# Two-layer graph attention on one core: the first weights' logit columns made by TensorE, the overflow flag computed between the last products, the last graph stored in pieces

## The chip, the cores and the metric

The kernel runs on one core of a Trainium2 chip. The metric is the device time of one launch in microseconds (us); lower is better. It is given as the median of several runs. Beside it stands one profiled execution, whose trace is what this document reads.

## The reference

There are 64 graphs of 256 nodes with 512 features each, an adjacency matrix of zeros and ones for each graph, and two residual layers. Everything is float32. Cut to what matters:

```python
# layer 0: two GAT layers inside (4 heads of 256, then 1 head of 512)
h  = relu(layernorm(x))
xl = (h @ W1).reshape(B, N, 4, 256)
a  = einsum(xl, att_src1); b = einsum(xl, att_dst1)      # one logit per node and head
e  = leaky_relu(a[source] + b[destination]); e = where(adj > 0 or diagonal, e, -1e9)
h  = elu(softmax(e, over sources) applied to xl + b1)    # 256 x 1024
...  the same with W2 (1024 x 512), one head, + b2
x  = x + h
# layer 1: one GAT layer with 8 heads of 64, softmax over neighbours, relu
h  = relu(layernorm(x));  xp = h @ W_proj
x  = x + relu(softmax(leaky_relu(a_src + a_dst + b_att), masked) @ xp)
```

A logit `einsum(xl, att)` of a head is linear in `h`, so it equals `h @ (W1_head @ att_head)`. The kernel computes the small vectors `W1_head @ att_head` once and puts them beside the weights as extra columns, the logit columns, so that a product gives the logits together with the features. For the first weights there are 4 source and 4 destination columns of 512 values.

## The kernel before

**Stages of a graph.** Each graph passes through products with W1 (`m1a` for heads 0 and 1, `m1b` for heads 2 and 3), attention (`gat1`), ELU, the product with W2 (`m2`), attention (`gat2`), a second normalization, the product with W_proj (`m3`) and attention (`gat3`). All of it is written as short named steps, and three strings `head`, `order` and `tail` list them in an order written out by hand: an entry such as `-1 m1a p6` is step `p6` of product `m1a` of graph r-1, and `w dots2 5` is a step on the weights. `head` runs once, `order` runs for r = 2 to 62, `tail` runs once with r = 64. Every engine gets its instructions in exactly this order and executes them in order; waits come only from data and from buffers.

**Products.** A product is done in seven smaller products of quarter matrices (`p1` to `p7`, class `Product`), which need sums and differences of the blocks of both sides. The sums on the side of the nodes are made by `left` on GpSimd (POOL), those of the weights by `right` on VectorE (DVE), once in the head (`sums1`, `sums2`, `sums3`). The steps `q1`, `q6`, `q7` copy a PSUM sum away on ScalarE (ACT), and `q2`, `c22`, `q3` add on VectorE and `q4` copies on ScalarE into `xl1`, `xl2` or `xl3`. A 128 x 512 PSUM tile for results comes from the pool `ps_mm` (name `pm`, four buffers); running sums come from `ps_sum` (two buffers).

**Logit columns of the first weights.** `dots1 0` to `dots1 7` on VectorE make 32 dot products of a weight block of 256 columns with an attention vector that was read from HBM into all 128 partitions. Each writes one column of `w1a_sb`. These columns ride only in `m1a`; `m1b` has none. `sums1 0` needs them; `sums1 1` does not. `dots2` and `dots3` make the columns of the other two weights.

**Attention.** `exp1` makes exponentials of the logits, `ship1` transposes them and sends them to HBM, `rows1` reads them back into all partitions (tile `bc`), `edges1` builds the attention matrix of a head with two ScalarE scalings into `wys` and two VectorE operations into `e`, `gat1` multiplies it with the features, and `out1` divides by the sum. Layers 2 and 3 have the same steps. The last graph does not go through HBM: `spread_at_once` makes the rows on TensorE.

**Turning.** TensorE needs the node features with the feature index on the partitions. Graph 0 is turned by TensorE (`turn0`), later ones through HBM (`away`, `home`) and VectorE (`back`); the last graph is turned by TensorE again in layer 3 (`back3` calls `turn`).

**Queues.** SyncE (SP) issues nearly all DMAs in order. ScalarE issues six of them at the start, and its two for the last two quarters of `w1a_sb` stand behind the normalization (`norm1`) in its queue. Every DMA signals on one of eight semaphores in turn, and a later DMA on the same semaphore is not issued until the earlier one has landed.

**The end.** `out3` divides on VectorE and adds into `x2` on GpSimd; `store` writes 512 KB for a graph. `range` keeps the largest and smallest exponential of a graph in `ends`. After the last step VectorE reduces `ends`, two tiny TensorE products sum over the partitions, and `flags` is written. All engines then read `flags` and branch around a slower general path, which is not taken with these inputs. The lines of the flag:

```python
    nc.vector.tensor_scalar(top[:, 3:4], top[:, 1:2], 1.0 / FAR, None, ALU.is_lt)
    pf = ps_mm.tile([P, 512], F32, name="pm")
    nc.tensor.matmul(pf[:2, 0:1], top[:, 2:4], ones, start=True, stop=True)
```

Of the kernel before, what the change touches and what calls it, by code (L numbers as in the profile page):

```python
# [110 lines left out]
def short_path(ctx, tc, flags, x, adj, w1, att_src1, att_dst1, b1, w2, att_src2, att_dst2, b2, w_proj, w_att,  # L111
# [51 lines left out]
    wp_sb = const.tile([P, 7, DC // 2, L3 + Q], F32, name="wp_sb")  # L163
    b1_sb = const.tile([P, HF], F32, name="b1_sb")
# [129 lines left out]
    class Graph:  # L294
# [264 lines left out]
        def out3(self, a, t):  # L559
            pv = self.pms.pop((3, a, t))[:, :G * (K3 + 1)].rearrange("p (h k) -> p h k", h=G)  # L560
            r = small.tile([P, G, 1], F32, name="r3")
            nc.vector.reciprocal(r, pv[:, :, K3:])
            o = work.tile([P, G, K3], F32, name="o", bufs=4)
            nc.vector.scalar_tensor_tensor(o, pv[:, :, :K3], 0.0, r.to_broadcast([P, G, K3]), ALU.max, ALU.mult)  # L564
            to = self.x2[:, t, a * Q:(a + 1) * Q]
            nc.gpsimd.tensor_tensor(to, to, o.rearrange("p h k -> p (h k)"), ALU.add)  # L566
# [5 lines left out]
        def store(self):  # L572
            nc.sync.dma_start(out[self.b].rearrange("(t p) d -> p t d", p=P), self.x2)
# [21 lines left out]
    def dot(dst, u, v):  # L595
        prod = work.tile([P, Q], F32, name="prod", bufs=2)
        nc.vector.tensor_tensor_reduce(prod, u, v, 1.0, 0.0, ALU.mult, ALU.add, dst)  # L597

    att1 = [work.tile([P, H1, F1], F32, name="x2", bufs=3) for i in range(2)]
# [4 lines left out]
    nc.scalar.dma_start(att1[0].rearrange("p h f -> p (h f)"), rows_of(att_src1, HF))  # L604
    for r in range(2):
        bring(w1_sb[1], w1, 2 * Q, r, (nc.sync, nc.scalar))
    nc.scalar.dma_start(att1[1].rearrange("p h f -> p (h f)"), rows_of(att_dst1, HF))
# [19 lines left out]
    class Weights:  # L627


        def __init__(self):  # L630

            self.dots = sorted(((r, s, h, c) for s in range(2) for r in range(2) for h in range(H1) for c in range(2)),
                               key=lambda d: (d[2] < 2, d[0] > 0 or d[2] % 2 == 0, d[1]))
            self.sums = {}

        def dots1(self, i):
            for r, s, h, c in self.dots[4 * i:4 * i + 4]:
                dot(blocks(w1_sb[0])[r][s][:, c, h:h + 1], blocks(w1_sb[h // 2])[r][h % 2][:, c, -Q:], att1[s][:, h, :])
# [5 lines left out]
        def dots2(self, i):  # L644
            r, c = i // 4, i % 4
            for s in range(2):
                for half in range(2):
                    dot(va2[:, i, s, half:half + 1], blocks(w2_sb)[r][half][:, c, -Q:],
                        att2[s][:, half * Q:(half + 1) * Q])
# [27 lines left out]


    head = """
        0 turn0, w dots1 0, w dots1 1, 0 m1b p2, w dots1 3, 0 m1b p1, w sums1 1, w dots1 4, w dots1 5, w dots1 6,  # L680
        0 m1a p1, w dots1 2, w dots1 7, 0 m1a p2, w dots2 1, 1 load, w dots2 3, w sums1 0, 0 m1a q1, 0 m1b q1,
        w dots2 0, 0 m1b p6, 0 m1a p5, 0 m1a q2, 0 m1b p5, w dots2 7, w load3, 0 edge01, 0 masks, 0 m1a p6,
        1 stats1 0, 0 m1b q6, 0 m1a q6, 0 m1a p7, 0 m1a q7, 0 m1a c22, w dots2 2, 0 m1a p3, 0 m1a q3, 0 m1a p4,
        0 m1b p7, 0 caps, w dots2 6, 0 m1a q4, 0 exp1, 0 ship1, w dots2 4, 1 stats1 1, w dots2 5, 0 m1b q7,
        0 rows1, w columns2, 0 m1b c22, 1 norm1 0, 1 norm1 1, 1 away1, w sums2 0, 0 m1b q2, 0 open, w sums2 1,
        0 edges1 1, w sums2 2, 0 m1b p3, 0 m1b p4, 0 cap3, 0 edges1 0, 0 gat1 1 1, 0 gat1 1 0, 0 out1 1 0,
        0 gat1 0 0, 1 home1, 0 gat1 0 1, 0 edges1 2, 0 out1 1 1, 1 edge01, 0 m1b q3, 1 masks, 0 out1 0 0,
        1 back1 0, 0 ez1 0 0, 1 m1b p1, 0 out1 0 1, w sums2 3, w dots3 1, 0 elu1 0 0, 1 caps, 0 m1b q4, 1 m1a p1,
        1 back1 1, 0 gat1 2 1, 0 gat1 2 0, w dots3 0, 2 load, 0 edges1 3, 0 ez1 0 1, 0 elu1 0 1, 0 gat1 3 1,
        0 out1 2 1, 0 out1 3 1, w dots3 2, 0 send2 0 0, 0 out1 2 0, 0 gat1 3 0, 0 out1 3 0, 1 m1a q1, 1 left1,  # L690
        1 m1a p6, 0 send2 0 1, 1 m1a p5, 1 open, 0 take2 0 1, 1 m1b q1, 0 ez1 1 1, 1 m1a p2, 1 m1a q6, 0 elu1 1 1,
        1 m1a q2, w dots3 5, 1 m1b p6, 1 m1a p7, 0 ez1 1 0, 0 send2 1 1, w dots3 7, 0 elu1 1 0, 1 m1b q6, 1 m1a q7,
        0 take2 0 0, 1 m1b p2, 1 m1b p7, 1 m1a c22, 1 m1a p3, 1 m1a p4, w dots3 4, 0 back2 0 1, 0 take2 1 1,
        0 send2 1 0, 1 m1a q4, 1 m1b p5, 0 back2 0 0, 1 m1b q7, 0 back2 1 1, 1 cap3, w dots3 3, 1 m1a q3,
        0 take2 1 0, 1 exp1, 1 ship1, 1 m1b p4, 0 m2 p1, 0 m2 q1, w dots3 6, w sums3 0, 0 back2 1 0, 1 m1b q4,
        0 left2, 0 m2 p5, 2 stats1 0, 1 m1b q2, 0 m2 p6, 2 edge01, 0 again, 1 m1b c22, 0 m2 p2, 1 rows1,
        2 stats1 1, 2 masks, 0 m2 q6, w sums3 1, 1 edges1 1, 0 m2 p7, 0 m2 q2, 1 edges1 0, 1 gat1 1 0, 1 gat1 1 1,
        0 m2 q7, 1 out1 1 1, 0 m2 p4, 0 m2 c22, 2 norm1 0, 0 m2 p3, 2 norm1 1, 1 m1b p3, w sums3 2, 1 out1 1 0,
        1 edges1 2, 1 gat1 0 1, w sums3 3, 0 m2 q4, 0 m2 q3, 2 caps, 1 edges1 3, 2 away1, 1 gat1 0 0, 0 exp2,
# [355 lines left out]
```

## Time and profile before

| what | value |
|---|---|
| median of 3 runs | 2969.14 us (2966.99 to 2972.52) |
| the profiled execution, its own time | 2968.22 us |
| its span in the profile | 2966.4 us |
| mean granted TensorE clock | 0.996 |
| TensorE (PE) busy | 2917.8 us, 98% of the span |
| VectorE (DVE) busy | 2531.3 us, 85% |
| ScalarE (ACT) busy | 1711.3 us, 58% |
| GpSimd (POOL) busy | 1287.4 us, 43% |

Times in the profile count from the start of the span. "Busy" is the time in which an engine executed something; an engine that is not busy is waiting or has nothing to do. A matrix product of float32 appears as two records for each instruction of the program. The columns of the views are named where they are shown.

### The profile page before, as it was taken

Reading aid. Unit: us, or ns where it says so; the run is one execution under the profiler, and the core shown is the slowest. Engines: PE = TensorE matmul, PEld = TensorE weight load, DVE = VectorE, ACT = ScalarE, POOL = GpSimd, SP = SyncE. Lnnn points to the kernel's source line nnn. Section 1 sums busy time; section 2 is a strip of 40 time slices with the busy share of each in tenths; the row PEclk is TensorE's granted clock in tenths of the full one; section 3 lists DMA queues with packets and bytes.
Section 4 is the critical chain, followed back from the end, with each engine's and each line's share of the span. In section 5 each row is a group of like instructions: output and inputs, shape, how many; then the busy total and the mean of one; then the engine's idle time right before and its main releaser. Section 6 shows DMA issues by size and latency. Waiting matters only on the chain.

```text
span 2966.4 us, 59522 instructions
## 1 busy us (share of the span) xinstructions
PE 2917.8 (98%) x20296; PEld 2531.6 (85%) x20296; DVE 2531.3 (85%) x6370; ACT 1711.3 (58%) x4489; POOL 1287.4 (43%) x1882
## 2 busy tenths in 40 slices
PE   6999999999999999999999999999999999999997
PEld 4888888888888888888888888888888888888886
DVE  8788888888888888888888888888888888888886
ACT  3466565655655655655656556556556556555554
POOL 3443443444444444434444444444444344344433
PEclk9999999999999999999999999999999999999998
DMA  6556555656565665555556565565555556566542
GB/s 193 155 173 180 175 180 171 180 178 179 170 182 176 175 180 174 172 180 177 179 171 185 173 179 173 178 184 167 175 177 174 178 178 179 172 182 176 179 136 73
DMA packets 536859, 513.17 MB, mean 173 GB/s; under 512 B 85736, under 2 KB 373352, under 8 KB 536552
## 3 DMA queue, kind: packets, MB, share of 16 engines
q1 hardware_dynamic: 535176, 507.20, 57.5%
q8 instruction: 165, 2.70, 0.4%
q10 hardware_dynamic: 1376, 2.10, 0.2%
q14 instruction: 142, 1.16, 0.1%
HBM read 332.01 MB, written 168.79 MB: 169 GB/s over the span
## 4 chain that ended last, share of the span: by engine, by line
PE 97%; DVE 1%; DMA 1%; issue 0%; ACT 0%; POOL 0%; SPq 0%; ACTq 0%; DVEq 0%
PE sum L55 38%; PE pm L55 29%; PE pm L411 15%; PE pm L556 8%; PE pm L481 7%; DVE prod L597 0%; DMA w1a_sb<-in_L_gnn_W_dram 0%; DMA xs<-in_x_dram 0%; DMA h<-kept_h 0%; DMA z<-kept_z 0%; DVE e L292 0%; DVE hs L213 0%; ACT h L199 0%; DVE z L419 0%; DMA bc<-kept 0%
## 5 line engine op out<-in xcount | busy, mean ns | idle before, releaser
L291 ACT ACTIVATE wys<-bc,exs_sb 128x256 f32<-128x256 f32 x1646 | 715.4, 468 | 297.4 <-DMA bc<-kept 145.4
L61 ACT ACTIVATE kept<-sum 128x260 f32<-128x260 f32 (+3 forms) x768 | 296.0, 386 | 714.0 <-PE sum L55 713.3
L292 DVE SCALAR_TENSOR_TENSOR e<-wys,exs_sb,cap 128x256 f32<-128x256 f32 x1024 | 444.9, 476 | 62.2 <-ACT wys L291 52.6
L55 PE MATMUL sum<-w_sb,h1s 128*128 128x257 f32 x2048 | 488.1, 380 | 0.6
L411 PE MATMUL pm<-xl,e 128*128 128x257 f32 x2048 | 476.4, 380 | 0.9 <-DVE e L292 0.8
L411 PEld LDWEIGHTS pm<-xl,e 128*128 128x128 f32 x2048 | 387.9, 190 | 60.1 <-DVE e L292 1.7
L55 PEld LDWEIGHTS sum<-w_sb,h1s 128*128 128x128 f32 x2048 | 383.3, 190 | 64.3 <-issue 3.8
L566 POOL TENSOR_TENSOR x<-x,o 128x256 f32<-128x256 f32 x256 | 182.0, 731 | 486.5 <-DVE o L564 484.6
L261 DVE TENSOR_TENSOR xl<-pm,kept 128x256 f32<-128x256 f32 (+2 forms) x768 | 318.1, 415 | 79.1 <-ACT kept L61 40.4
L219 POOL TENSOR_TENSOR hs<-hs 128x256 f32<-128x256 f32 x128 | 109.0, 852 | 617.9 <-DVE hs L213 589.8
L55 PE MATMUL pm<-w_sb,h1s 128*128 128x257 f32 x1536 | 361.6, 384 | 0.0
L55 PEld LDWEIGHTS pm<-w_sb,h1s 128*128 128x128 f32 x1536 | 285.8, 189 | 44.8 <-POOL h1s L219 1.0
L213 DVE STREAM_TRANSPOSE hs<-h 128x512 f32<-128x512 f32 x252 | 283.2, 1150 | 8.4 <-DMA h<-kept_h 8.0
L292 DVE SCALAR_TENSOR_TENSOR e<-wys,exs_sb,mask 128x256 f32<-128x256 f32 x640 | 278.4, 477 | 12.9 <-ACT wys L291 7.0
L449 DVE STREAM_TRANSPOSE h1s<-z 128x512 f32<-128x512 f32 x252 | 260.6, 1104 | 17.6 <-DMA z<-kept_z 17.6
L55 PE MATMUL sum<-w1a_sb,hs 128*128 128x260 f32 x1024 | 269.1, 386 | 4.0 <-DVE w1a_sb L597 3.4
L55 PE MATMUL sum<-wp_sb,hs 128*128 128x264 f32 x1024 | 271.0, 387 | 0.7 <-ACT hs L229 0.7
L55 PE MATMUL sum<-w1b_sb,hs 128*128 128x256 f32 x1024 | 266.4, 383 | 4.9 <-DVE r L417 2.6
L556 PEld LDWEIGHTS pm<-xl,e 128*64 128x64 f32 x8192 | 245.9, 138 | 24.8 <-issue 24.1
L419 DVE SCALAR_TENSOR_TENSOR z<-pm,r,b_sb 128x256 f32<-128x256 f32 x512 | 247.7, 484 | 18.3 <-DVE r L417 0.3
L219 POOL TENSOR_TENSOR h1s<-h1s 128x512 f32<-128x512 f32 x64 | 81.3, 1270 | 412.2 <-DVE h1s L449 405.2
L556 PE MATMUL pm<-xl,e 128*64 128x65 f32 x8192 | 255.8, 223 | 1.9 <-DVE e L292 1.7
(94 smaller groups left out, 4832.0 us busy)
## 6 DMA issues: line engine op xcount, KB each, us to landing
bc<-kept SPq DMA_DIRECT2D x380, 256.0 KB, 4.6
kept_h<-h SPq DMA_DIRECT2D x126, 512.0 KB, 3.5
h<-kept_h SPq DMA_DIRECT2D x126, 512.0 KB, 3.7
kept_z<-z SPq DMA_DIRECT2D x252, 256.0 KB
z<-kept_z SPq DMA_DIRECT2D x252, 256.0 KB, 2.9
xs<-in_x_dram SPq DMA_DIRECT2D x64, 512.0 KB, 6.0
x<-in_x_dram SPq DMA_DIRECT2D x64, 512.0 KB
out_dram<-x SPq DMA_DIRECT2D x64, 512.0 KB
```

The lines of the kernel that those rows point to most:

```text
L55: self.nc.tensor.matmul(to[:, :self.n], self.lhs[:, i, c, :], self.rhs[:, i, c, :], start=(first and c == 0), stop=(last and c == self.nk ...
L61: self.nc.scalar.activation(s[:, :self.n], self.sum[:, :self.n], AF.Copy)
L213: nc.vector.transpose(a[:, 4 * t:4 * t + 2].rearrange("p r k (j q) -> p q (r k) j", q=4), h[:, t].rearrange("p (q i c) -> p q c i", q=4, c=4))
L219: nc.gpsimd.tensor_tensor(s1, s3, a22, ALU.add)
L261: nc.vector.tensor_tensor(dst, pm, add, ALU.add)
L291: nc.scalar.activation(wy, bc, AF.Copy, scale=yw)
L292: nc.vector.scalar_tensor_tensor(dst, wy, xw, mask, ALU.max, op)
L411: nc.tensor.matmul(pm[:, :Q + 1], self.e[1, h][:, s, t * P:(t + 1) * P], xl1[:, s, h, L1:], start=(s == 0), stop=(s == T - 1))
L419: nc.vector.scalar_tensor_tensor(self.zt[t][:, sl], pm[:, :Q], r, b1_sb[:, sl], ALU.mult, ALU.add)
L449: nc.vector.transpose(a.rearrange("p k (j q) -> p q k j", q=4), z.rearrange("p (q i c) -> p q c i", q=4, c=4))
L481: nc.tensor.matmul(pm[:, :n], self.e[2][:, s, t * P:(t + 1) * P], xl2[:, s, half, L2:L2 + n], start=(s == 0), stop=(s == T - 1))
L556: nc.tensor.matmul(pv[q:q + 64, h, :], self.e[3, a * G + h][:, s, t * P + q:t * P + q + 64], xl3[:, s, a * G + h, :], start=(s == 0), stop ...
```

## The change

Four things are changed; the `order` string is the same.

1. `dots1` and its two broadcast loads (512 KB each) are gone. The eight attention vectors are loaded as 16 rows of 128 (`vec_sb`). `lay` turns them on TensorE and ScalarE lays them out with zeros between (`va1`). `turnw u` turns four 128 x 128 blocks of W1 on TensorE, and ScalarE copies them to SBUF. `dotw u` multiplies by them (8 columns kept, 512 moved) and sums over the eight u. `cols` copies the 8 x 512 sum, turns it back with four small transposes and writes it into the blocks of `w1a_sb` with four ScalarE copies.
2. The flag's operations are now steps `top`, `pair` and `flag` of the weights, listed in the tail among the last graph's steps.
3. For the last graph `out3` adds on VectorE instead of GpSimd and issues a 128 KB store for each of its four pieces; `store` does nothing for it.
4. The `head` and `tail` lists are new throughout. In the new head no product stands ahead of `cols`, and in the new tail `range` of the last graphs stands ahead of their `edges3`.

`dots2` writes its unused product into another scratch name.

```diff
+    vec_sb = const.tile([16, P], F32, name="vec_sb")
+    va1 = const.tile([P, 8, 2, H1], F32, name="va1")
+    nc.gpsimd.memset(va1, 0.0)
...
-            nc.gpsimd.tensor_tensor(to, to, o.rearrange("p h k -> p (h k)"), ALU.add)
+            (nc.gpsimd if self.gone else nc.vector).tensor_tensor(to, to, o.rearrange("p h k -> p (h k)"), ALU.add)
+            if not self.gone:
+                nc.sync.dma_start(out[self.b, t * P:(t + 1) * P, a * Q:(a + 1) * Q], to)
...
+    nc.scalar.dma_start(vec_sb[0:8, :], att_src1.rearrange("h (i f) -> (h i) f", f=P))
+    nc.scalar.dma_start(vec_sb[8:16, :], att_dst1.rearrange("h (i f) -> (h i) f", f=P))
-    nc.scalar.dma_start(att1[0].rearrange("p h f -> p (h f)"), rows_of(att_src1, HF))
-    nc.scalar.dma_start(att1[1].rearrange("p h f -> p (h f)"), rows_of(att_dst1, HF))
...
-        def dots1(self, i):
-            for r, s, h, c in self.dots[4 * i:4 * i + 4]:
-                dot(blocks(w1_sb[0])[r][s][:, c, h:h + 1], blocks(w1_sb[h // 2])[r][h % 2][:, c, -Q:], att1[s][:, h, :])
+        def lay(self):
+            pm = ps_mm.tile([P, 512], F32, name="pm")
+            nc.tensor.transpose(pm[:, :16], vec_sb, ident[:16, :16])
+            for j in range(2):
+                for h in range(H1):
+                    nc.scalar.activation(va1[:, 2 * h:2 * h + 2, j, h], pm[:, 8 * j + 2 * h:8 * j + 2 * h + 2], AF.Copy)
+        def turnw(self, u):
+            pm = ps_mm.tile([P, 512], F32, name="pm")
+            for c in range(4):
+                src = blocks(w1_sb[u // 4])[c // 2][(u // 2) % 2]
+                at = src.shape[2] - Q + (u % 2) * P
+                nc.tensor.transpose(pm[:, c * P:(c + 1) * P], src[:, c % 2, at:at + P], ident)
+            self.wt[u] = work.tile([P, 512], F32, name="e", bufs=9)
+            nc.scalar.activation(self.wt[u], pm, AF.Copy)
+        def dotw(self, u):
+            if u == 4:
+                self.acc = ps_sum.tile([P, 512], F32, name="sum")
+            nc.tensor.matmul(self.acc[:2 * H1, :], va1[:, u].rearrange("p j h -> p (j h)"), self.wt.pop(u),
+                             start=(u == 4), stop=(u == 3))
+        def cols(self):
+            m = 2 * H1
+            flat = work.tile([P, 512], F32, name="e", bufs=9)
+            nc.scalar.activation(flat[:m], self.acc[:m, :], AF.Copy)
+            pm = ps_mm.tile([P, 512], F32, name="pm")
+            for c in range(4):
+                nc.tensor.transpose(pm[:, c * m:(c + 1) * m], flat[:m, c * P:(c + 1) * P], ident[:m, :m])
...
     head = """
-        0 turn0, w dots1 0, w dots1 1, 0 m1b p2, w dots1 3, 0 m1b p1, w sums1 1, w dots1 4, w dots1 5, w dots1 6,
-        0 m1a p1, w dots1 2, w dots1 7, 0 m1a p2, w dots2 1, 1 load, w dots2 3, w sums1 0, 0 m1a q1, 0 m1b q1,
+        w turnw 4, 0 turn0, w turnw 6, w turnw 7, w lay, w turnw 5, w turnw 0, w turnw 1, 0 edge01, w dotw 4,
+        w dotw 5, w sums1 1, w dotw 6, w dotw 7, w dotw 0, w turnw 2, w dotw 1, w turnw 3, w dotw 2, w dots2 3,
+        w dotw 3, w cols, w dots2 1, 0 m1a p1, w dots2 0, 0 m1a p2, 0 masks, 0 m1a q1, w sums1 0, 0 caps, 0 m1b p1,
+        0 open, 1 load, 0 m1b q1, 0 m1a p6, w dots2 6, 0 m1a q6, 0 m1a p5, 0 m1a p7, w dots2 7, 0 m1a q7,
+        0 m1a c22, w dots2 4, 0 m1b p6, 0 m1a p4, 0 m1a p3, 0 m1b p2, 0 m1a q3, 0 m1b q6, 1 stats1 0, 0 m1a q2,
+        0 m1b p7, 0 m1a q4, 0 exp1, 0 cap3, 0 ship1, 1 stats1 1, w dots2 2, 0 m1b q7, 0 m1b q2, w load3, 0 rows1,
...
     tail = """
-        -1 edges3 2, -1 edges3 3, -1 edges3 6, -3 store, -1 edges3 1, -1 edges3 0, -1 edges3 5, -1 edges3 4,
-        -1 gat3 0 0, -1 out3 0 0, -1 send2 1 0, -1 edges3 7, -1 gat3 0 1, -1 gat3 1 0, -2 store, -1 out3 0 1,
-        -1 out3 1 0, -1 gat3 1 1, -1 out3 1 1, -1 store, -1 range, -2 range, -1 take2 1 0
+        -1 batt3, -1 exp3, -1 range, -1 edges3 7, -1 edges3 4, -1 edges3 5, -1 edges3 6, -3 store, -1 edges3 1,
+        -1 edges3 0, -1 gat3 1 1, -1 gat3 1 0, -1 out3 1 1, w top, -1 edges3 2, -1 edges3 3, -1 out3 1 0, -2 store, -1 gat3 0 0,
+        w pair, -1 gat3 0 1, -1 out3 0 0, w flag, -1 out3 0 1
```

## The prediction

> **What bounds the kernel now.** First the page: the span, the busy shares and the chain that ended last.
>
> ```profile
> span 2966.4 us, 59522 instructions
> ...
> PE 2917.8 (98%) x20296; PEld 2531.6 (85%) x20296; DVE 2531.3 (85%) x6370; ACT 1711.3 (58%) x4489; POOL 1287.4 (43%) x1882
> ...
> PE 97%; DVE 1%; DMA 1%; issue 0%; ACT 0%; POOL 0%; SPq 0%; ACTq 0%; DVEq 0%
> ```
>
> PE sets the time, and it idles for only 48.6 us. The table of stretches says where (start:end, length, then busy us of PE, PEld, DVE, ACT, POOL, clock, DMA share, GB/s):
>
> ```profile
> 20.00:30.00 10.00, 5.91 (x12) 3.69 (x12) 9.97 (x57) 1.04 (x3) 0.00 (x0) 1.00 1.07 361
> ...
> 40.00:50.00 10.00, 5.52 (x19) 4.27 (x18) 9.93 (x41) 4.83 (x13) 1.48 (x4) 0.83 0.32 97
> ...
> 60.00:70.00 10.00, 10.00 (x48) 8.55 (x47) 9.86 (x27) 4.81 (x11) 9.92 (x13) 1.00 0.49 135
> ...
> 400.00:2400.00 2000.00, 1999.13 (x13968) 1739.79 (x13967) 1725.28 (x4298) 1179.72 (x3100) 875.49 (x1281) 1.00 0.59 177
> ...
> 2920.00:2940.00 20.00, 14.83 (x142) 11.98 (x141) 12.73 (x35) 10.79 (x27) 5.81 (x11) 0.83 0.22 82
> ```
>
> The middle, whose list is unchanged, has no gap to win. In the head DVE is full from 20 us on and PE waits for it. So only the head and the last 50 us can move, and an earlier head moves everything behind it one for one. Next the chain in the head (start, length, what):
>
> ```profile
> 11.78 7.79 DMA w1a_sb<-in_L_gnn_W_dram
> 19.59 0.42 DVE prod L597
> 20.02 0.34 DVE prod L597
> ```
>
> The first products wait for weights, then for dots on them. From PE's timeline (start, length, instruction, count, idle before and who ended it):
>
> ```profile
> 21.46 2.10 PE L55 MATMUL sum<-w1a_sb,hs 128*128 128x260 f32 x4 [3.42 <-DVE w1a_sb L597]
> ...
> 56.21 1.81 PE L55 MATMUL sum<-w1b_sb,hs 128*128 128x256 f32 x4 [2.57 <-DVE r L417]
> 57.81 1.94 PE L55 MATMUL sum<-w1a_sb,hs 128*128 128x260 f32 x4
> 59.54 3.83 PE L411 MATMUL pm<-xl,e 128*128 128x257 f32 x16
> ```
>
> A dot costs DVE 0.345 us. A pass of 256 columns takes 0.217 us, but 0.43 for about 3.5 us after the 2.57 us gap: PE then runs at half rate. The clock column (1.00 in 20 to 30) does not show it in every row; the passes do. Last, the end:
>
> ```profile
> 2953.94 3.23 PE L556 MATMUL pm<-xl,e 128*64 128x65 f32 x96
> ...
> 2958.76 0.37 SPq L573 DMA_DIRECT2D out_dram<-x  x1
> ...
> 2959.93 0.15 DVE L793 TENSOR_SCALAR flags<-pm 1x1 int32<-1x1 f32 x1 [0.28 <-PE pm L792]
> ```
>
> From the last product (2957.2) to the flag (2960.1) it takes 2.9 us, and from there to the end 6.3.
>
> **Removed from the head.** 32 dots: 32 x 0.345 = 11.0 us of DVE. Two 512 KB loads: 2.9 us of DMA at the 361 GB/s above, out of the way of the weights; two 4 KB loads replace them.
>
> **Added: the gate t0.** In the new list all 14 products of graph 0 stand behind `cols` on PE. Before, `m1b p2` and `p1` ran at 14.3 and `m1a p1` at 21.46, so I work out t0, the start of the new `m1a p1`.
> - ACT gets to the copies at S. It normalizes graph 0 when `xs` is there (6.8 before; in the first 4 us ScalarE's loads took 0.39 of the 0.50 MB moved, so 5.3 to 6.8 now), 5.0 us later it is through (6.8 to 11.78), and then issues two DMAs of `w1a_sb`, the second of which waited until 13.2 for an earlier quarter. All copies are queued behind these issues. S lies between 11.1 and 13.6; I take 11.8, since 1 MB less is ahead of that quarter.
> - Five 128x512 copies (`turnw` 4, 6, 7 and the two of `turn0`) at 0.55 (the two `hs` copies take 1.08): 2.75. PE's four transposes take 1.0 cold (eight in 1.98) and lie beside this. Then `lay`: eight tiny copies, nearest the three `exp1` instructions in 0.44, so 0.15 each: 1.2. With 0.3 of hand-overs `dotw 4` starts at 16.1.
> - The dots on PE: nothing in the trace moves 512 columns. Two passes of 256 take 0.435, so a `dotw` is 0.87, eight are 7.0; two late `turnw` are 4 x 0.12 = 0.5 each (warm): 24.1. Cold throughout, the dots and these two cost 7.9 more. I charge one cold stretch of 3.5 us as at 56.21, which loses 1.75: 25.8.
> - `cols`: one copy 0.55, four transposes 0.4, four tiny copies 0.7, hand-overs 0.5: 2.2. So **t0 = 28.0**, between 25.5 and 36.
> - The last quarters of `w1a_sb` landed at 19.6; `turnw 2` is not reached before 20.5, so they are hidden. If they came later than that, each us would cost one.
>
> The Trainium skill ("TensorE: Matmul & The Clock Gate", Part 1) says that the clock halves only after an idle window of about 3.4 us and returns after about 3.4 us of work. The row with 2.57 us of idle contradicts the first figure. By the rule the transposes from 10 us on would have PE warm for the dots, and the time would be 1.75 us below the forecast.
>
> **From t0 to the first `gat1`.** Before, from `m1a p1` (21.46) to `gat1` (49.76) it took 28.3 us, stretched by the dots on DVE. Now DVE has, until `exp1`: `sums1 0` 2.8, three `dots2` at 4 x 0.345 = 4.15, three additions 1.05, statistics 0.9, so 8.9; PE's ten products need 8.7 beside it; with waits 9.7, and `exp1` 0.44. From there to the first `wys` took 6.6 us (41.67 to 48.27, ACT being busy last) and 5.35 in the tail (2921.9 to 2927.25): I take 6.0. Two `wys` and an `e` make 1.4. First `gat1` at t0 + 17.5 = 45.5 against 49.76.
>
> **The rest of the head.** PE needed 46.5 us from there to the end of `2 m1b p1` at 96.28, of which its 180 passes of 0.217 are 39.1. DVE was busy 44.2 of these 46.5, so DVE sets it. Its work there is the same except one more `sums2` (1.2), and 1 us of waiting: 46.4. The head ends at 91.9 instead of 96.28: **-4.4 us**. What is late next is DVE again, one `out1` after the other.
>
> The other moves there: `cap3` (SP busy 3.06 us) now stands ahead of `ship1`, and `load3` ahead of `rows1`. `open` is done at t0 + 4, so `cap3` has left SP by t0 + 7, before `ship1` at t0 + 10; 512 KB of `load3` pass in 1.4 us while `rows1` waits 1.9 us for `ship1` to land. Nothing, with that cover; otherwise up to 3 and 1.4. `dots2`'s scratch name and the memset on POOL: nothing, POOL idles there.
>
> **The tail.** PE's work is the same. `norm3 1` now directly follows `norm3 0` on ACT, so the second `turn` and POOL's four sums (2935.53 before) come up to 3 us earlier; but PE idles little between 2929 and 2944 (0.8 us), so I take 0.4 of that. Then the eight last `edges3`: 1.06 us each, 2945.42 to 2955.41 with a 1.2 us hole for `spread_at_once`. In the new list the hole is filled, but `out3 1 1` with its add on DVE and `top` (1.1 + 0.6) stand between edges 6 and 7 on DVE, and `edges3` behind them: 8.5 + 1.3 = 9.8. After that DVE does three `out3` with their adds (0.18 + 0.42 + 0.35 and hand-overs, 1.1 each), `pair` and `flag` (0.4), then SP's store 0.4 and its read of the flag: 14.0 after the start of the edges, where the old flag came 14.66 after it. That gains 0.6, if the 6.3 us count from SP; if they count from the flag alone, 2.2; if DVE is held once more, -0.7. The POOL add that goes (0.73 and 0.2) is inside this sum. **Tail -1.0**, between -2.6 and +1.
>
> **Sum:** 2968.2 - 4.4 - 1.0 = 2962.8 for an execution like the profiled one. The median stands 0.9 above it, so **2963.7**. A measurement can tell about 0.2% here (5.9 us), so this lies just at the edge.
>
> **Rivals.**
> - *TensorE bounds the rest of the head.* For it: DVE's 8 us of `dots3`, `sums2` and `sums3` are not needed at once, and the new list may let PE pass them. Against: DVE was full for 50 us. Then 39.1 + 2 instead of 46.4, 5.3 less: 2958.4.
> - *The gate is late.* PE stays cold through all dots, as it did from 30.8 to 36.3, and ACT comes at 13.6: t0 = 34. Against: 7 us of contiguous transposes ahead. 6 us more than forecast: 2969.7, no change. Break-even is at t0 = 33.4.
> - *Slower: the additions of the first products stand behind `dots2` on DVE* as they did before, when 19.8 us passed from `m1a p1` to `exp1`. For it: `dots2` 6, 7 and 4 are still between them in the list. Against: only 12 dots are left where 40 stood. Each us over 9.7 costs one; over 15.1 it is slower than before, and from 21.0 on it is slower by over 0.2%.
> - *The end does not follow the flag*, but something after the store; then the tail gives 0.4 instead of 1.0, inside the range.
>
> **How the numbers follow.** Forecast 0.50 (own range 2960 to 2967), TensorE-bound 0.15, late gate 0.23, slower 0.12. Faster by over 0.2% (below 2963.2): 0.15 and just over half of the forecast's half, 0.42. Slower by over 0.2% (above 2975.1): 0.10, most of the last case, where a late gate can add to it. The rest, 0.48, is within 0.2%. The range reaches from the TensorE-bound case less 1 to the late gate plus 1.3: 2957.4 to 2971.
>
> **What would show it.** Right: no `prod L597` in the chain, `m1a p1` near 28, first `gat1` near 45.5, `2 m1b p1` or its equal near 92, flag before the last `out3`. Wrong: a `dotw` near 1.7 us, PE idle over 4 us between `cols` and `gat1`, or a gap between 100 and 2920, where there was none.

## The result, and the profile after

The changed kernel takes 2965.43 us in the median of 22 runs (2959.34 to 2968.29); the kernel before took 2969.62 us in 22 runs beside it. The ratio is 0.9981 with a 95% interval of 0.9975 to 0.9987, so the change gains 4 to 6 us: the medians lie 4.2 us apart, the ratio stands for 5.6. The forecast was 2963.7 us, with 2957.4 to 2971.0. The total is right; several of the steps that make it up are not, and they err in opposite directions, so it is right in part by luck.

The profiled execution took 2968.29 us, the slowest of the 22 and no shorter than the one profiled before. The page of after:

```profile
span 2966.6 us, 59581 instructions
PE 2926.8 (99%) x20349; PEld 2536.3 (85%) x20349; DVE 2519.1 (85%) x6310; ACT 1718.1 (58%) x4510; POOL 1283.0 (43%) x1879
```

PE is busy 9 us longer than before: the 53 new passes over the weights took 13.4 us, and fewer other passes of the head ran slowly. VectorE is busy 12 us less. The same stretches as before (start:end, length, busy us of PE, PEld, DVE, ACT, POOL, clock, DMA share, GB/s):

```profile
20.00:30.00 10.00, 8.82 (x38) 5.74 (x38) 7.96 (x34) 4.20 (x15) 0.80 (x1) 1.00 0.72 233
40.00:50.00 10.00, 9.24 (x30) 7.43 (x30) 8.47 (x22) 7.69 (x19) 2.56 (x5) 0.68 0.57 183
...
400.00:2400.00 2000.00, 1996.51 (x13949) 1737.83 (x13948) 1721.97 (x4287) 1178.72 (x3097) 875.04 (x1281) 1.00 0.59 177
```

VectorE is no longer full, but the granted clock fell to 0.68 in the stretch from 40 us, and in the middle, whose list is unchanged, PE was busy 2.6 us less than before. PE's timeline of after shows where PE waits in the head and for whom (start, length, instruction, count, idle before and its releaser):

```profile
14.23 4.46 PE L656 MATMUL sum<-e,va 128*8 128x512 f32 x10
...
23.99 1.14 PE L55 MATMUL sum<-w1a_sb,hs 128*128 128x260 f32 x4 [0.27 <-ACT w1a_sb L669]
...
38.86 1.41 PE L55 MATMUL pm<-w1b_sb,hs 128*128 128x256 f32 x4 [2.81 <-DVE xl L264]
41.02 9.84 PE L414 MATMUL pm<-xl,e 128*128 128x257 f32 x32 [0.76 <-DVE e L295]
...
63.93 2.07 PE L55 MATMUL sum<-w1b_sb,hs 128*128 128x256 f32 x4 [2.52 <-ACT kept L61]
...
91.92 1.97 PE L484 MATMUL pm<-xl,e 128*128 128x257 f32 x8 [2.84 <-DVE e L295]
...
122.34 3.05 PE L414 MATMUL pm<-xl,e 128*128 128x257 f32 x12 [2.73 <-DVE e L295]
```

The first `gat1` starts at 41.0 instead of 49.8, but its passes are slow (9.84 us for 32, where 32 x 0.217 would be 6.9), and four single waits of 2.5 to 2.8 us follow one another. The last two are in the first pass of the repeated list. Before, PE did not wait at the place of the wait at 92 us, and the place of the last one had 0.83; it waited 2.20 for VectorE near the end of the head:

```profile
95.31 1.13 PE L55 MATMUL sum<-w1b_sb,hs 128*128 128x256 f32 x4 [2.20 <-DVE hs L213]
...
125.95 3.05 PE L411 MATMUL pm<-xl,e 128*128 128x257 f32 x12 [0.83 <-DVE e L292]
```

In the chain of after, the middle has a wait that no event explains (start, length, what):

```profile
1240.76 3.23 PE pm L559 x105
1243.99 2.58 issue
1246.58 0.92 PE pm L559 x23
1247.49 5.36 PE pm L55 x16
```

The end, from VectorE's timeline of after:

```profile
2960.05 0.15 DVE L728 TENSOR_SCALAR flags<-pm 1x1 int32<-1x1 f32 x1 [0.35 <-PE pm L727]
...
2960.85 0.42 DVE L569 TENSOR_TENSOR x<-x,o 128x256 f32<-128x256 f32 x1
```

The flag is written 6.4 us before the end of the span, as it was before (6.35), although an addition and a store follow it now.

### The profile page after: what moved, and what is told of

It reads as the page before. It is cut to its first block, busy times and chain, and to the rows that moved or that the text cites. A ratio compares the mean times of both kernels' runs of the same rounds, so it can differ in the third digit from the quotient of the medians.

```text
span 2966.6 us, 59581 instructions
## 1 busy us (share of the span) xinstructions
PE 2926.8 (99%) x20349; PEld 2536.3 (85%) x20349; DVE 2519.1 (85%) x6310; ACT 1718.1 (58%) x4510; POOL 1283.0 (43%) x1879
## 3 DMA queue, kind: packets, MB, share of 16 engines
q8 instruction: 166, 2.72, 0.4%
## 4 chain that ended last, share of the span: by engine, by line
PE 97%; DMA 1%; DVE 1%; POOL 0%; ACT 0%; issue 0%; ACTq 0%; DVEq 0%; POOLq 0%; SPq 0%
PE sum L55 37%; PE pm L55 28%; PE pm L414 15%; PE pm L559 8%; PE pm L484 7%; PE sum L656 0%; DMA bc<-kept 0%; DVE e L295 0%; DMA h<-kept_h 0%; DMA z<-kept_z 0%; ACT wys L294 0%; DMA xs<-in_x_dram 0%; PE pm L649 0%; PE pm L231 0%; DVE stats L188 0%
## 5 line engine op out<-in xcount | busy, mean ns | idle before, releaser
L55 PEld LDWEIGHTS pm<-w_sb,h1s 128*128 128x128 f32 x1536 | 286.8, 190 | 45.5 <-POOL h1s L222 1.2
```

The costliest lines, as they stand in the source:

```text
L55: self.nc.tensor.matmul(to[:, :self.n], self.lhs[:, i, c, :], self.rhs[:, i, c, :], start=(first and c == 0), stop=(last and c == self.nk ...
```

## The experiments

Each kernel was timed beside the kernel before on its chip, whose median was 2967.4 to 2967.8 in all four groups. Single executions lie up to 6 us from their kernel's median, and the intervals of the ratios reach about 0.0009 to each side, so a difference of 1 us between two experiments says nothing by itself; the places in the traces do.

**1. The changed kernel once more** (no edit).

> The changed kernel once more, with nothing altered. In its first profile it led the kernel before by 3.1 to 4.3 us from 190 to 1240 us, lost 4.3 at 1244 us where TensorE waited 2.58 us for nothing that the profile shows and then ran a product at half rate, and came out level at the end. Theory 1 (that stall is chance and belongs to single executions): the new profile has no stall at 1244, or one at another place, its span is about 4 us shorter (2962 to 2963), and the median gain is 4 to 7 us. Rival (the stall is bound to the place in the program): it is at 1244 again, and the span is 2966 to 2967.

Measured: 2962.94 us, ratio 0.9986 (0.9977 to 0.9995). The profile has no wait at 1244 us; its span is 2963.3. Theory 1 holds for this profile. The place is not chance, though: in four of the seven other profiles with the new head and no products added ahead of it, a wait of 0.6 to 1.4 us came back there; its length is what changes. How the lead over the profiled execution of before runs through the program (start of the same step in both, us):

| kernel | at 100 | at 151 | at 2806 | end of span |
|---|---|---|---|---|
| after | -6.0 | -4.2 | +1.9 | +0.1 |
| after, once more | -3.9 | -1.3 | -0.3 | -3.1 |
| new head only (2) | -4.8 | -2.1 | -0.4 | +0.1 |
| old end (4) | -4.8 | -2.5 | -3.1 | -5.4 |
| new tail only (3) | +0.4 | -0.1 | -1.5 | -4.4 |

So the head gains 3.9 to 6.0 us up to 100 us and loses 1.9 to 2.7 of that by 151; the middle drifts from execution to execution, by -1.5 to +6; the new tail gains 1.8 to 2.9 after 2806.

**2. and 3. Head alone, tail alone.** The old list `tail` with the old end behind the new head, and the new `tail`, flag and stores behind the old head:

```diff
-    tail = """ (new list) """        # 2: new head only
+    tail = """ (list of before) """, out3 adds on GpSimd, one store, flag behind run(tail, B)
-    head, dots1, att1 (new)          # 3: new tail only
+    head, dots1, att1 of before
```

> The new head and logit columns with the tail, the flag and the single store of the kernel before. Theory 1 (the head brings 3 to 4 us, the tail and the end the rest, about 2): 2965 to 2966 us, 3 to 4 us less than before. Rival A (the head brings nearly all, as predicted 4.4 of 5.4): 4.4 us less or more. Rival B (the new head's lead of 6 us at 100 us is lost in the handover to the old list at 122 us, and what the runs show comes from the end): within 2 us of before.

> The old head with its 40 dots on VectorE, and the new tail: its list, the flag between the last products, the additions of the last graph on VectorE and its four stores. Theory 1: 1.5 to 2.5 us less than before (the lead in the profile grew by 2.2 us after the last attention of layer 2). Rival A (the predicted 1.0): 0.5 to 1.5 less. Rival B (the gain at the end is a chance of one profile): no difference, within 0.5.

Measured: head alone 2965.76 us (0.9993, 0.9984 to 1.0002), 1.6 less than before; tail alone 2965.06 us (0.9992, 0.9983 to 1.0001), 2.3 less. Together 3.9, against 4.5 for both in this group. Each interval is 2.7 us wide on either side, so the medians alone tell neither from no change, and they do not decide between the theories: the head's 1.6 lies under theory 1's 3 to 4 and inside rival B's 2 us, the tail's 2.3 inside theory 1. The table decides more. It speaks against rival A of both, since 1.3 to 4.2 us of the head's lead are left at 151 us and the tail gains 1.8 to 2.9, over the predicted 1.0 in each of four profiles. Of rival B of the head half is right: the handover takes 1.9 to 2.7 us, not all.

**4. The new tail list with the old end.**

```diff
-            (nc.gpsimd if self.gone else nc.vector).tensor_tensor(to, to, o..., ALU.add)
-            if not self.gone: nc.sync.dma_start(out[...], to)
+            nc.gpsimd.tensor_tensor(to, to, o..., ALU.add)
...
-        ..., w top, ..., w pair, ..., w flag, ...        # the flag behind run(tail, B) again, one store
```

> The changed kernel with the new list of the tail, but with the old end: additions of the last graph on GpSimd, one store of the last graph, and the flag's work after all products. It tells the list of the tail from the edits at the end. Theory 1 (the end is worth about 2 us, since with the flag out of the way the program ends 5.3 us after the last addition): 2 us slower than the changed kernel. Rival (the list itself brings what the tail brings, and the program's end does not follow the flag): within 0.7 us of the changed kernel.

Measured: 2962.46 us (0.9985, 0.9976 to 0.9994), 0.5 below the changed kernel: the rival holds for its first half. The three edits of the end bring nothing that can be seen; the list does. From the first of the last eight `edges3` to the written flag it took 14.7 us before and 14.7 with the new head alone, but 12.7 with the new list and the old end, and 12.8 in after; from the flag to the end of the span it took 5.8 to 6.4 in all four. The list has two parts in this. It puts both `range` steps (four reductions on VectorE) ahead of these edges; VectorE's timeline with the old list (new head alone) has them between the last `out3` and the flag's first step:

```profile
2958.15 0.42 DVE L567 SCALAR_TENSOR_TENSOR o<-pm,r 128x256 f32<-128x256 f32 x1
2958.49 0.30 DVE L572 TENSOR_REDUCE ends<-exs_sb 128x1 f32<-128x148 f32 x1
...
2959.35 0.21 DVE L832 TENSOR_REDUCE top<-ends 128x1 f32<-128x64 f32 x1
```

With the new list and the old end there is nothing between:

```profile
2953.19 0.42 DVE L567 SCALAR_TENSOR_TENSOR o<-pm,r 128x256 f32<-128x256 f32 x1
2953.53 0.21 DVE L832 TENSOR_REDUCE top<-ends 128x1 f32<-128x64 f32 x1
```

That is 0.8 us. And the last product ends 10.5 us after the first edge instead of 11.8. The new end gives the latter back: with the additions on VectorE it is 11.6 to 12.6 in the nine profiles with the new list and the new end up to experiment 10, while in after the flag follows the last product by 0.3 us instead of 2.1.

**5. Does VectorE bound the head?** The 32 products of layer 2's weights left out.

```diff
         def dots2(self, i):
-            (four tensor_tensor_reduce of 256 columns)
+            nc.vector.memset(va2[:, i], 0.0)
```

> The changed kernel without the 32 products of layer 2's weights with its attention vectors on VectorE (11 us of VectorE in the head, between 22 and 65 us); layer 2's logit columns are left at zero, the memsets in their place cost 0.5 us. Theory by the prediction (VectorE sets the rest of the head): first gat1 2 us or more earlier than 41 to 43 us, the lead at 100 us 4 to 8 us larger. Rival (the head waits for round trips and for the order on ScalarE and GpSimd; VectorE is full but with work that is not needed yet): first gat1 and the lead at 100 us move by less than 2 us, and the gaps at 64 and 92 us stay. In both cases the time may gain less than the lead at 100 us, as the wait at 122 us takes from it.

Measured: 2960.77 us (0.9980, 0.9971 to 0.9989). In the windows VectorE (third number) is far from full, and PE still waits:

```profile
20.00:30.00 10.00, 8.82 (x38) 5.13 (x37) 2.82 (x6) 4.79 (x16) 0.80 (x1) 1.00 0.65 213
30.00:40.00 10.00, 8.01 (x36) 6.28 (x34) 4.99 (x18) 3.46 (x9) 2.19 (x4) 1.00 0.34 99
```

PE's timeline and the chain of the same run:

```profile
42.24 10.17 PE L414 MATMUL pm<-xl,e 128*128 128x257 f32 x32 [4.11 <-DVE e L295]
```

```profile
35.17 2.02 DMA kept<-wt
...
37.21 3.82 DMA bc<-kept
...
41.11 0.49 ACT wys L294
```

With 11 us less on VectorE the first `gat1` came at 42.2 (41.0 to 43.1 with them), 17.4 us after the first product, and the lead at 100 us was 4.7. So VectorE's load does not set the first `gat1`: a round trip of 5.8 us through HBM takes its place here. The rival holds. From the first `gat1` to the end of the head this run takes nothing away, since the last of the 32 products ran at 38 us in after. What sets that stretch is read from the windows from the first `gat1` to the first product of the repeated list (columns as above; in order before, after, this run and experiment 11):

```profile
49.76:96.28 46.52, 41.74 (x182) 34.80 (x181) 44.16 (x101) 24.93 (x63) 27.82 (x34) 0.96 0.49 141
41.02:87.17 46.15, 43.63 (x180) 36.95 (x181) 41.87 (x98) 24.64 (x61) 27.59 (x34) 0.90 0.43 133
42.24:88.83 46.59, 44.07 (x181) 37.43 (x182) 41.82 (x98) 24.61 (x61) 27.58 (x34) 0.90 0.43 132
42.55:86.06 43.51, 40.15 (x180) 33.79 (x181) 41.77 (x98) 24.59 (x61) 27.74 (x34) 1.00 0.45 141
```

In after 180 passes at 0.217 make 39.1 us, slow passes add 4.4 and the wait for ScalarE at 64 us 2.5: 46.0 of the 46.15. Experiment 11 runs the same stretch at full rate and is 2.6 us shorter with the same work on VectorE. So VectorE is not the bound there either. That the median was 2 us below the changed kernel has no place in the trace up to 151 us; this stays open.

**6. The wait at 122 us: back3 later.** In the first pass of the list only:

```diff
-  0 gat1 0 1, -2 back3 0, -2 back3 1, 1 caps, -1 bias 1, 0 gat1 1 0, -1 m2 q2, 0 edges1 3, 1 norm1 0,
+  0 gat1 0 1, 1 caps, -1 bias 1, 0 gat1 1 0, -1 m2 q2, 0 edges1 3, -2 back3 0, -2 back3 1, 1 norm1 0,
```

> The changed kernel, with one edit in the first pass through the repeated list only: the two transposes of graph 0 for layer 3 (back3, which wait on VectorE for the read of home3) stand behind the fourth edges1 of graph 2 instead of three steps ahead of it. In the four profiles of the new head the lead over the kernel before falls at 122 us from 3.6 to 5.5 us to 0.7 to 3.6 us: VectorE waits there for home3 while the e of the next gat1 is queued behind. Theory (that wait takes 2 to 3 us of the head's gain, since the round trip of graph 0 starts only 2 us earlier than before while TensorE comes 4 to 5 us earlier): the gap of 2.2 to 2.7 us at 122 us and the half rate behind it are gone, the lead at 150 us is 4 to 5 us, and the kernel is 2 to 3 us faster than the changed kernel. Rival (the next step of TensorE waits for the same trip, so the gap only moves to m3 p1): a gap as long within 5 us, and the same time.

The chain of the second run of the changed kernel shows what it was about:

```profile
94.33 3.52 DMA kept_z<-z
97.91 4.24 DMA z<-kept_z
...
103.45 1.28 POOL h1s L222
...
108.91 0.71 POOL rstd L194
...
111.77 3.47 DMA kept_h<-h
115.26 5.65 DMA h<-kept_h
```

This is graph 1's trip into layer 2, GpSimd's four sums for it, and behind them on GpSimd the rstd of graph 0, whose own trip follows. In that run GpSimd's sums start only 2.2 us earlier than before (103.45 against 105.61), while PE is 3.9 us ahead. Measured: 2962.57 us (0.9986, 0.9977 to 0.9995). The lead fell from 5.6 us at 120 only to 4.3 at 140, by 1.3, where the same products lost 1.9 to 3.1 in the four profiles above; the theory holds on the place. But the time is that of the changed kernel within its scatter (the middle of this execution lost 1.4 at 1240 us again), so the 2 to 3 us of the expectation were not seen in the median.

**7. cap3 out of SP's way.**

```diff
-  head:  ..., 1 out1 3 1, 2 cap3, 1 out1 2 1, ...
+  first pass of the list:  ..., -1 send2 1 1, -1 take2 0 0, 0 cap3, 0 m1b q1, ...
```

> The changed kernel with cap3 of graph 2 (two transposing DMAs that hold SP for 2.8 us at 90 us) moved from the end of the head behind the last three sends of graph 1 in the first pass of the repeated list. The trace of the wait at 122 us leads back over home3, away3, norm3, GpSimd's four sums of left2, and a read and a write of z that SP issues after cap3. Theory (SP's queue is a link of that trip): the write of z is issued 1 to 3 us earlier, the gap at 122 us shrinks by as much, and the kernel is 1 to 2.5 us faster than the changed kernel. Rival (the trip is set by VectorE's elu1 or by the statistics of graph 0, SP is no link): the gap stays over 2 us and the time is the same within 0.5 us.

Measured: 2964.23 us (0.9987, 0.9978 to 0.9996); the wait at 122 us is 2.51 us, the lead falls from 6.2 to 3.0. By these numbers the rival holds. The edit took `cap3` only halfway out of the way, however: SP issued it at 91.9 us, still ahead of the last two reads of z, and GpSimd's sums began 0.9 us earlier than in after (100.67 against 101.52). So for this move SP's queue is worth under 1 us; whether a larger one would gain is open.

**8. Where do the waits of the middle come from?** Products ahead of all work.

```diff
+    pad = ps_mm.tile([P, 512], F32, name="pm")
+    for i in range(64):
+        nc.tensor.matmul(pad[:1, i:i + 1], ones, ones, start=True, stop=True)
```

> The changed kernel with 64 products of one column ahead of all TensorE work, in the first 7 us in which TensorE idles: 128 instructions more, which shift all that follows by half a block of 256 instructions (16 KB, the size in which the trace shows TensorE's instructions arriving). In the profiles gat3 of a middle graph (128 short passes, 256 instructions in 3.4 us) stalls only where it starts 226 to 251 instructions behind a multiple of 256. Theory (a stall happens where a block ends late in such a gat3, since the next takes about 4 us to come): no stall any more at 247, 744, 1241, 2644 and 2735 us; stalls of 0.2 to 0.9 us, now and then of 2 to 3, at some of 699, 790, 1196, 1290, 1696, 2192 and 2690 us; the time is within 1.5 us of the changed kernel. Rival (the stalls belong to these graphs, by their other transfers): they stay at 247 and 744 us.

The edit did not do what the text says: a float32 product ran as two passes with a load each (128 passes in the trace), so the shift was 256 instructions, a whole block, and by the count of records one more. A `gat3` also takes 3.9 us by the rows below, not 3.4. Measured: 2963.86 us (0.9988, 0.9979 to 0.9997). PE's timeline of this run: the `gat3` at 248 us, which stalled in all seven other profiles of the new head up to here, runs through, and others stall:

```profile
248.24 3.95 PE L559 MATMUL pm<-xl,e 128*64 128x65 f32 x128
...
1647.45 3.60 PE L559 MATMUL pm<-xl,e 128*64 128x65 f32 x114
1651.61 0.57 PE L559 MATMUL pm<-xl,e 128*64 128x65 f32 x13 [0.56 <-issue]
```

So the stalls do not belong to fixed graphs (the rival falls): they move with the instructions ahead of them, and in experiments 11 and 12, which add passes too, the places at 247 and 744 us run through as well. The phase theory is not shown. Four of its five places run through (at 2641 us 0.2 is still lost), none of the seven that it named instead stalls, and a shift of one block and one instruction should have moved them little. Over the 13 other profiles the time of the middle `gat3` above its median of 3.88 us sums to 0.5 and 0.7 us with the old head and 1.3 to 5.6 with the new one. Why the old one's are fewer is open, with two profiles of it.

**9. One exchange on ScalarE.**

```diff
-        2 norm1 1, 1 m1b q7, 0 take2 1 0, 2 norm1 0, ...
+        1 m1b q7, 2 norm1 1, 0 take2 1 0, 2 norm1 0, ...
```

> The changed kernel with two neighbours of the head's list exchanged: the copy q7 of m1b of graph 1 stands ahead of the second norm1 of graph 2 on ScalarE. In all profiles of the new head TensorE idles 2.5 us at 64 us for that copy, which is queued behind a norm1 that waits for rstd on GpSimd. Theory 1 (the head is a row of such single waits, none of them VectorE's load): the gap of 2.5 us is gone, the half rate behind it too, and the lead at 90 us grows from 4.2 to 6.6 us by 2.5 to 4; the waits at 92 and 122 us, which end on round trips, take most of it back, so that the time gains 0 to 1.5 us. Rival (TensorE's next products wait for VectorE as well): the gap moves by less than 1.5 us and the lead at 90 us stays.

Measured: 2961.90 us (0.9981, 0.9972 to 0.9990), 1 us below the changed kernel of the first group. In its timeline the wait at 64 us is 0.47 and the products behind run at full rate; a wait of 2.77 at 92 us stands as before:

```profile
62.21 1.13 PE L55 MATMUL sum<-w1b_sb,hs 128*128 128x256 f32 x4 [0.47 <-ACT kept L61]
...
92.18 1.97 PE L484 MATMUL pm<-xl,e 128*128 128x257 f32 x8 [2.77 <-DVE e L295]
```

The lead at the step that before starts at 73 us was 9.8 us, against 7.2 in after. By 90 us it was 6.3, against 6.6 in after, and by 103 us 5.8. So theory 1 holds for the gap and for the time, and fails for the lead at 90 us: the gain was gone before the wait at 92. PE's next products waited 0.70, 1.31 and 0.44 us for results of VectorE, as the rival says; the 1.31 ends on an `e` whose rows (`bc`) came from HBM at 68.9 us, 2.3 later than in after. Experiment 10, which has the same exchange, kept 1.7 us of it to the end of the head.

**10. Both moves.** The exchange, and `back3` of graph 0 behind two `out1` (in front of `1 norm1 1`).

> The exchange of q7 and norm1 in the head together with back3 of graph 0 moved behind two out1 of graph 2 in the first pass of the repeated list (in an earlier run, with back3 only one e later, 1.3 of the 2.9 us were still lost, since an out1 that frees a PSUM buffer stood behind it on VectorE). Theory: no wait over 0.8 us at 122 us, the lead at 150 us is 4.5 to 7 us, and the time is 1.5 to 3.5 us below the changed kernel: 2959.5 to 2962. Rival (a trip of graph 0 sets the first pass, whatever is moved): a wait of 2 us or more appears within 15 us behind, and the time is that of the changed kernel.

Measured: 2964.39 us (0.9990, 0.9981 to 0.9999), no gain: the rival holds. ScalarE's second `norm1` of the next graph writes the tile `h`, of which there is one buffer and which `back3` reads; moved back, `back3` keeps ScalarE from it, and the `wys` behind it. That is read from the code. The trace fits it: VectorE's two transposes of `back3` end at 121.74 us, and ScalarE's `norm1` starts at 121.90. The chain of this run has the wait, without a releaser, and PE's timeline what it costs:

```profile
116.60 5.21 issue
121.90 1.52 ACT h L202 x2
```

```profile
125.42 2.19 PE L414 MATMUL pm<-xl,e 128*128 128x257 f32 x8 [2.96 <-DVE e L295]
```

**11. Unread work that keeps the clock up.** 20 transposes into a PSUM tile that nobody reads then, in PE's idle time ahead of `m1b p5`.

```diff
+    for i in range(20):
+        nc.tensor.transpose(wys[1][:, i % 2 * P:(i % 2 + 1) * P], ident, ident)
```

> The changed kernel with 20 transposes that nobody reads (2.4 us of TensorE) in the idle time ahead of m1b p5 of graph 0, at 36 to 39 us. In the records the clock is granted in windows of 3.41 us, and the window behind one in which TensorE was busy for 42% or less ran at half rate, in every profile so far; ahead of the first gat1 that cost two windows in each profile of the new head (6.8 us at half rate). Theory: with the dummies the window at 36 to 39 us is over 45% busy, there is no half rate between 38 and 50 us, the first eight gat1 take 7.0 to 7.5 us instead of 9.8 to 10.2, and the lead at 56 us grows by 2 to 3.4 us; the wait at 64 us, which does not depend on TensorE, takes most of it, so the time gains 0 to 1 us. Rival (the clock falls by idle time as such, 2 us or more without real products, or by something else): half rate stays at 40 to 49 us.

Measured: 2959.35 us (7 runs, 2958.19 to 2961.00), ratio 0.9973 (0.9961 to 0.9984): the lowest median here, though its interval overlaps with those of the changed kernel (0.9981 and 0.9986). All its runs lie at or below 2961.0; of the 33 runs of the changed kernel, on other chips, two do. The windows of the clock in after:

```profile
36.16:39.57 3.41, 0.71 (x3) 0.66 (x4) 3.41 (x17) 1.52 (x2) 0.86 (x3) 1.00 0.84 279
39.57:42.99 3.42, 2.66 (x7) 1.61 (x7) 2.36 (x6) 2.61 (x7) 1.22 (x2) 0.50 0.59 178
42.99:46.40 3.41, 3.41 (x10) 2.67 (x9) 3.11 (x9) 1.97 (x6) 0.78 (x2) 0.50 0.85 290
```

and with the 20 transposes:

```profile
35.43:38.85 3.42, 3.42 (x27) 3.24 (x26) 3.38 (x16) 0.75 (x4) 1.76 (x4) 1.00 0.38 115
38.85:42.26 3.41, 1.98 (x8) 1.07 (x7) 2.81 (x13) 2.19 (x4) 0.00 (x0) 1.00 0.91 284
42.26:45.67 3.41, 3.12 (x13) 2.39 (x14) 3.37 (x11) 2.73 (x8) 2.01 (x3) 1.00 0.35 101
```

No half rate is left between 35 and 86 us, and the first 32 passes of `gat1` take 7.63 instead of 9.84 us. The lead at 150 us was 5.2, against 0.7 to 3.6 by the same product in the four profiles of the new head above. I had expected the wait at 64 us to take most of it. The theory was right on the clock; by the median it was too low on the worth, which experiment 12 does not repeat.

**12. The same in three places.** 18 more ahead of graph 0's `gat2`, 32 behind the last `gat2`.

```diff
-  first pass:  -2 gat2 0,
+  first pass:  w warm 18, -2 gat2 0,
-  tail:  -1 gat2 1, -2 rows3,
+  tail:  -1 gat2 1, w warm 32, -2 rows3,
```

> The changed kernel with unread transposes in three idle times of TensorE: the 20 of the run before at 36 us, 18 ahead of gat2 of graph 0 at 88 us (where a window 39% busy cost one at half rate behind it), and 32 behind the last gat2 in the tail at 2920 us (4.2 us of idle for norm3 of the last graph, then two windows at half rate over the turns and the first products of m3). Theory (windows under about 43% busy are followed by one at half rate): none of the half rate left before the last product, the two turns and m3 p1 and p2 in the tail take 3 us instead of 5.9, and the time is 1.5 to 3.5 us below that of 20 dummies alone: 2956 to 2958. Rival (the first products of the last graph wait for the round trip or for ScalarE and VectorE anyway): the tail ends as before, and the time is 2958.5 to 2960.

Measured: 2962.47 us (0.9981, 0.9972 to 0.9990), 3 us worse than with 20 alone, so both forecasts of the time fail; three of its eleven runs are as fast as those. In the tail of the profiled execution (2959.04 us) the theory holds, with the turns and `p1` and `p2` of m3 in 4.0 us instead of 5.7:

```profile
2919.95 3.66 PE L675 MATMUL sum<-ident 128*128 128x128 f32 x32
2924.34 1.45 PE L231 MATMUL pm<-ident,h 128*128 128x128 f32 x8 [0.73 <-ACT h L202]
2926.32 1.16 PE L55 MATMUL sum<-wp_sb,hs 128*128 128x264 f32 x4 [0.53 <-ACT hs L232]
2927.32 1.05 PE L55 MATMUL pm<-wp_sb,hs 128*128 128x264 f32 x4
```

The 18 failed: they stand behind `edges2` in the list and write a tile that its `e` reads, so they came after the idle time that they were meant to fill, and in front of `gat2`.

```profile
90.35 2.19 PE L675 MATMUL wys<-ident 128*128 128x128 f32 x18 [2.87 <-DVE e L295]
```

Why the other executions were up to 5 us longer than the profiled one is open. This run holds the 20 transposes of experiment 11 too, so the worth of those rests on one group of seven runs and on their trace.

## Why the prediction was right, step by step

- **The gate t0.** Predicted 28.0; measured 23.6 to 25.6 in the twelve profiles with the new head, all but one under the lower bound of 25.5. In after `dotw 4` started at 14.2 instead of 16.1, since ScalarE reached the copies at 10.0 instead of 11.8 and the eight tiny copies took 0.62 instead of 1.2. The dots and their last turns took 8.4, not 9.7: the cold stretch of 3.5 us that I charged (1.75) was not there, five `dotw` at 0.89 each. `cols` took 1.4, not 2.2. The cold stretch was wrong because PE had worked without a gap from 9.3 on. The Trainium skill ("TensorE: Matmul & The Clock Gate", Part 1) says that full rate returns after about 3.4 us of work; that half of its rule fits these rows, and I had set the whole rule aside for one row.
- **From t0 to the first gat1.** Predicted 17.5; measured 17.0 in after, up to 17.7 in the others and 17.4 without `dots2`: right, and its terms too (in after 10.6 us to the end of `exp1`, 5.3 to the first `wys` and 1.1 to `gat1`, against 10.1, 6.0 and 1.4). The forecast of 45.5 was late by the error of t0 and little else.
- **The rest of the head.** Predicted 46.4 from the first `gat1` to the head's end; measured 46.15 in after and 46.0 to 46.6 in eight others (43.5 to 44.4 in experiments 10 to 12). The number came out by luck, since the step behind it, "DVE sets it", failed. Before, two waits that ended on VectorE (2.57 and 2.20 us) were in that stretch. They are gone; a wait for ScalarE (2.52) and 2 us more of slow passes stand in their place (experiment 5).
- **Where the head's lead went.** With the early gate the head ended 9.1 us earlier in after (87.17 against 96.28), not 4.4. Then came a wait that the prediction does not have: the first product of `gat2` stands behind `ship2`'s round trip, 2.84 us at 92 us, where PE did not wait before. The lead at 100 us, 3.9 to 6.0 and in the mean 4.9, is near the predicted 4.4 because this wait gave back what the gate had gained too much.
- **"An earlier head moves everything behind it one for one".** This failed. At 122 us 1.9 to 3.1 us went back (the fall of the lead from 119 to 143 us in the four profiles) to a trip through HBM, GpSimd and HBM again whose sums on GpSimd had started only 2.2 us earlier in the profile shown. I had listed a gap between 100 and 2920 as a sign of being wrong, and given it no price.
- **The middle.** I took it as unchanged. Its list is, but it lost 1 to 6 us in three of four profiles with the new head. That its instructions lie elsewhere in the stream is the likely reason (experiment 8), not a shown one.
- **The tail.** Predicted 1.0, measured 2.3 alone and 1.8 to 2.9 in the traces. The 14.0 us to the last store were right (13.8 to the last addition), but the end counts from the flag, which was the other end of my bound (2.2), and I had not seen that the list moves `range` (0.8). From the last `gat2` to the first edge the new list gave 0.4 in the two profiles in which two windows ran at half rate there, as before, and 1.3 and 1.5 in the two with one such window: the 0.4 that I had for norm3 was right, and the rest is the clock. The rival that the end does not follow the flag falls: over all 14 profiles it takes 5.8 to 7.0 us from the flag to the end, and 4.9 to 7.7 from the issue of the last store.
- **The other rivals.** That TensorE bounds the rest of the head was nearer than my forecast: it waits once there, but with slow passes of 4.4 us that the rival did not have, so its 2958.4 did not come. The late gate did not come, and the additions of the first products did not stand behind `dots2` long enough to matter (17.0 against 17.4 us).

## What to carry to other kernels

When a start is made earlier, look for the first round trip behind it that does not start earlier by as much, and price the wait there; a busy engine is the bound only where the waiting one waits for its last result, which taking work from it in that very stretch shows. Where TensorE idles for a known wait, a little unread work in that wait can keep its clock up; what that is worth in the end has to be measured more than once. And read two or three profiles of a kernel before explaining one: here a single profile said "no gain" for a kernel that gains 4 to 6 us.

## What the runs showed of the hardware

- **The clock goes by windows, not by gaps.** The granted clock changes at multiples of 3.413 us, and where the windows lie differs from execution to execution. In the first 150 us of the 14 profiles, each of the 30 windows at full rate in which PE was busy for 41% or less was followed by a window at half rate; every window with 44% or more by one at full rate; of two between, at 42 and 43%, one went either way. A window at half rate was followed by another one when PE was busy for 53 to 79% of it (11 times, counted from the first window at full rate on), and by full rate from 85% on: in work done that is the same bound, about 0.42 of what a window can do. So an idle time of 2.5 to 2.8 us can cost nothing, one slow window or two, depending on where it falls. In after the wait at 92 us cost none, the one at 64 us a window, and the one at 39 us two (9.84 us for passes that take 6.9 at full rate). At 122 us the wait left 45% in after and no half rate, 36% in its second run and a window at half rate. The Trainium skill ("TensorE: Matmul & The Clock Gate", Part 1) gives an idle window of about 3.4 us as the condition and the same window length; the runs agree on the length, not on the idle share.
- **PE's instructions seem to come in blocks that short passes can outrun.** The page of after lists 166 packets on an instruction queue (2.72 MB, 16 KB each), one for about 253 of PE's records; experiment 8, with 257 records more, has 167. Waits for "issue" in the middle lie in `gat3` alone, where 128 passes of 65 columns and their loads go by in 3.9 us, after 98 to 123 of the passes; most took 0.2 to 0.8 us, a few 1.1 to 2.6, the longest with a window at half rate behind it. That a late block is the cause is inferred, not tested.
